# Opening loads in one queue, dummy matmuls in the opening, and a reordered last store in an adapter and mixture-of-experts kernel

## The chip, the cores and the metric

The kernel runs on one core of one Trainium2 chip. A core has five engines that run beside each other: TensorE (PE) for matrix products, VectorE (DVE), ScalarE (ACT), GpSimd (POOL) and SyncE (SP), which here only issues transfers, and 16 DMA engines that move the data. The metric is the device time of one execution in microseconds (us); less is better.

## What is computed

4,096 tokens (16 batches of 256, width 256) pass through an adapter that each batch chooses by an id, a layer norm, a shared feed-forward block and a mixture of eight experts, of which each token uses two. Cut to what matters:

```python
z = relu(einsum('bsh,bhk->bsk', x, down_w[ids]) + down_b[ids])
y = x + einsum('bsk,bkh->bsh', z, up_w[ids]) + up_b[ids]
h = (y - mean(y)) * rsqrt(var(y) + 1e-5) * ln_g[ids] + ln_b[ids]

def mlp(x, w1, b1, w2, b2):            # 256 -> 1024 -> 256
    return gelu(x @ w1 + b1) @ w2 + b2

p = softmax(h @ gate_w + gate_b)       # 8 experts
values, indices = top_k(p, 2)          # then divided by their sum
moe = sum over the two experts of value * mlp_e(h)
out = x + h + mlp_shared(h) + moe
```

All inputs and outputs are float32. The kernel gets float32 accuracy from f16 matmuls by splitting every operand into a high and a low part and multiplying three of the four pairs.

## The kernel before

**Stages.** For each batch `b`, the adapter computes z (L865, two f32 products), relu (L875), up (L881, and L885 for the bias row) and y (L896); `adapter_ln` does the layer norm (L922 to L961), `payload` splits the result into two f16 parts (L984, L989), transposes them on PE (L1000) and copies them to `xlnT` (L1008), and multiplies by the gate weights (L1019). `route` finds the two experts of each token for two batches at a time, and POOL scatters their rows into `xslot` in DRAM (L1139, 64 scatters). Beside that, `shared` runs the shared expert for one batch after another: 8 groups of 6 matmuls with W1 (L689), gelu on ACT (L696), a split into parts (L704 or L706, and L710), 8 groups of 6 matmuls with W2 (L725), and an eviction that adds to `base` (L1392). 13 of the 16 batches are done before the experts, the last three after them. The experts follow in units of 256 tokens: 16 at fixed places (two for each expert), then 16 whole and 5 half ones whose expert is found at run time. Each unit's blocks come by transposing loads on SP (L1281), and its weighted results are added to `yacc` in DRAM by POOL (L1303). At the end `yacc` is loaded back (L1607), added to `base` (L1627) and stored (L1615), batch by batch.

**Weights.** `Prep` loads one expert's f32 weights in two halves of about 1 MB (`load`, L539), sums their squares on ACT (L555), adds these up across partitions on PE (L578), computes scales on DVE (L585 to L603), and writes the scaled f16 high parts on ACT (L638) and the low parts on DVE (L644). `pE` is the `Prep` of the shared expert; its result is `wsh`. In the opening its two halves are issued from ACT's queue, after the load of adapter weights of batch 0 and of batch 1.

**The order of the work.** Nothing is ordered by hand. Every step is a `plan.op` with an engine, an assumed duration, a due time `v`, the steps that it needs (`deps`), steps that have to start before it (`after`), and buffers that it takes and gives back. `Plan.schedule` goes through a planned time: of all steps that are ready it takes the one that can start first, and among equals the one due first. The kernel then emits all steps in that order, so each engine's queue has a fixed order, and an engine stands still while the step at the head of its queue waits. The planned time is only used for the order. Due times come from a few numbers: `PACE` (start and step of the adapters, start and step of the shared units), `P_V` (the first two experts' weights), `VE2` (the shared expert's second half), `TV` and `WV` (how long before a unit its blocks and its weights are due), `PU2` (step of the expert units).

**The opening.** `load_batch` issues four loads of 256 KB for a batch from SP: the transposed input `xT` (L842), the adapter weights (L832, whose address comes from the id), the input `x` (L849) and the rows for the layer norm (L839). ACT's queue has the bias rows, the ids, the tables `gb_t` and `gw32` of the layer norm and the gate, the gate's bias and the shared expert's weights. `x_scales` turns the maxima of these tables into scales; it uses PE twice (transpose L470, spread L481). `constants` starts with 28 matmuls of a tile of ones into a bank of PSUM (`N_WARM`, L316).

Of the kernel before, what the change touches and what calls it, by code (L numbers as in the profile page):

```python
# [19 lines left out]
P = 128  # L20
NB = 16
# [3 lines left out]
E = 8  # L25
# [4 lines left out]
BLK = 256  # L30
# [25 lines left out]
X_FROM = 5  # L56
HALF_AT = (2, 5, 8, 11, 14)
# [91 lines left out]
P_V = (100.57, 91.12)  # L149
PACE = (0.0, 10.1, 24.89, 16.04)  # L150
VE2 = 3.67
TV, WV, PU2, VP = 9.48, 22.84, 10.68, 1.4
# [3 lines left out]
def adapter_moe_kernel(  # L156
# [16 lines left out]
    V, ACT, PE, POOL, SP = nc.vector, nc.scalar, nc.tensor, nc.gpsimd, nc.sync  # L173
# [15 lines left out]
    base = const([P, NTILE, D], F32, "base")  # L189
# [325 lines left out]
    class Prep:  # L515
# [29 lines left out]
        def build(self, joint=True, bank_of="pt"):  # L545
# [85 lines left out]
            for h, o in ((0, O_W1), (1, O_W2)):  # L631
                his = []
                for i in range(2):
# [17 lines left out]
                    his.append(plan.op("ACT", 1.1, hi, vh, [t[h], *sq[h:]] + gate[h]))  # L651
# [165 lines left out]
    z_of, ln_done, tc_done, lo_of, gate_of = {}, {}, {}, {}, {}  # L817
# [40 lines left out]
    def adapter_pe(b):  # L858
# [4 lines left out]
        def z():  # L863
# [7 lines left out]
            "PE", 0.86, z, va, [ld["xT"][b], ld["wa"][b]], acq=[("pt", ("z", b))], lat=0.3  # L871
# [21 lines left out]
        )  # L893
        return plan.op(
# [452 lines left out]
    gbl = plan.op("ACT", 0.45, lambda: ACT.dma_start(gb_t, lngb), 0.03, land=P * 128)  # L1347
    gwl = plan.op("ACT", 0.45, lambda: ACT.dma_start(gw32, gate_w), 0.03, land=P * 64)
    hot_first, hot_all = profile_rows()
    load_batch(0, 0.0, [])  # L1350
    pE = Prep(E, 2.3, after=[gwl], v2=VE2)
    pE.ld = [pE.load(0, 0.25, "ACT")]
    pE.ld[0]["after"] = [ld["wa"][0]]
# [4 lines left out]
    pE.ld.append(pE.load(1, 1.5, "ACT"))  # L1358
    pE.ld[1]["after"] = [pE.ld[0], ld["wa"][1]]
# [254 lines left out]
    def store(b, eng=SP):  # L1614
        eng.dma_start(  # L1615
            out[b * S : (b + 1) * S, :].rearrange("(t p) d -> p t d", p=P),
            base[:, 2 * b : 2 * b + 2, :],
        )
# [6 lines left out]
    def sum_y(b):  # L1625
        bb = base[:, 2 * b : 2 * b + 2, :]
        V.tensor_tensor(bb, bb, y_buf[b], ALU.add)  # L1627

    for b in range(NB):
        ld_y = plan.op(  # L1630
            "SP", 0.5, lambda b=b: y_load(y_buf[b], 2 * b, 2), v_end + b,
            [sc_last[NU - 1], *ring_free], land=P * 2048,
        )
        o = plan.op(
            "DVE", 0.69, lambda b=b: sum_y(b), v_end + 4.0 + 1.5 * b,
            [ld_y] + (last_evac[b] if b < NSH else []),
        )
        plan.op("SP", 0.5, lambda b=b: store(b), v_end + 9.0 + 1.5 * b, [o, *last_evac[b]])

    order = plan.schedule()  # L1640
    with tc.manual_schedule():
        constants()
        for o in order:
            o["fn"]()
# [117 lines left out]
```

## Time and profile before

| | |
|---|---|
| median of three runs | 628.97 us (628.46 to 629.08) |
| the profiled execution, its own time | 629.32 us |
| span in its profile, first to last instruction | 627.5 us |
| granted TensorE clock over the span, mean | 0.974 |
| PE busy | 599.8 us (96%) |
| DVE busy | 402.6 us (64%) |
| ACT busy | 412.3 us (66%) |
| POOL busy | 327.9 us (52%) |
| one group of six matmuls, L689 or L725, at full clock | about 0.66 us |
| DMA traffic | 129.30 MB, mean 206 GB/s |

In the profile an engine is busy while one of its instructions runs; PE's matmuls are pipelined. "PEclk" is the share of full speed that PE's clock was granted. The "chain that ended last" is followed back from the last instruction, at each step to what released it. A pair such as `wst<-in_adp_dram` is destination and source of an operation, without buffer numbers: `wst` also holds the adapter weights and rows in the opening. "SPq" and "ACTq" are the sequencers that issue transfers.

### The profile page before, as it was taken

Reading aid. Unit: us, or ns where it says so; the run is one execution under the profiler, and the core shown is the slowest. Engines: PE = TensorE matmul, PEld = TensorE weight load, DVE = VectorE, ACT = ScalarE, POOL = GpSimd, SP = SyncE. Lnnn points to the kernel's source line nnn. Section 1 sums busy time; section 2 is a strip of 40 time slices with the busy share of each in tenths; the row PEclk is TensorE's granted clock in tenths of the full one; section 3 lists DMA queues with packets and bytes.
Section 4 is the critical chain, followed back from the end, with each engine's and each line's share of the span. In section 5 each row is a group of like instructions: output and inputs, shape, how many; then the busy total and the mean of one; then the engine's idle time right before and its main releaser. Section 6 shows DMA issues by size and latency. Waiting matters only on the chain.

```text
span 627.5 us, 15396 instructions
## 1 busy us (share of the span) xinstructions
PE 599.8 (96%) x5541; PEld 521.1 (83%) x5541; DVE 402.6 (64%) x1005; ACT 412.3 (66%) x627; POOL 327.9 (52%) x541
## 2 busy tenths in 40 slices
PE   4799999999999999999999999999999999999993
PEld 3478877887888888888888888898898989889882
DVE  5698879898985338667777743444554555444464
ACT  1378765878787578788898766665565566555550
POOL 2005775662688326648446648564545844846300
PEclk7589999999999999999999999999999999999998
DMA  7856765975733378599999999656997499783297
GB/s 256 282 219 234 250 170 203 339 269 187 281 116 111 57 165 196 101 287 283 201 235 311 211 318 228 183 68 199 268 242 195 62 304 210 187 202 38 33 302 240
DMA packets 100315, 129.30 MB, mean 206 GB/s; under 512 B 56558, under 2 KB 83846, under 8 KB 92038
## 3 DMA queue, kind: packets, MB, share of 16 engines
q1 hardware_dynamic: 84210, 108.08, 58.6%
q0 software_dynamic: 15216, 18.01, 16.0%
q10 hardware_dynamic: 804, 2.16, 1.0%
q8 instruction: 45, 0.74, 0.5%
q14 instruction: 40, 0.33, 0.2%
HBM read 92.41 MB, written 46.58 MB: 222 GB/s over the span
## 4 chain that ended last, share of the span: by engine, by line
PE 87%; ACT 4%; DVE 4%; DMA 2%; issue 1%; SPq 0%; ACTq 0%; DVEq 0%
PE bank L689 40%; PE bank L725 40%; PE bank L881 3%; PE bank L865 2%; DMA wst<-in_adp_dram 1%; DVE base L1627 1%; PE bank L885 1%; PE bank L1000 1%; ACT h L696 1%; DVE hh L710 1%; DMA wst<-in_rows_dram 1%; PE bank L1019 1%; ACT wst L638 1%; ACT wsh L638 1%; ACT hh L704 1%
## 5 line engine op out<-in xcount | busy, mean ns | idle before, releaser
L725 PEld LDWEIGHTS <-hh 128*128 128x128 f16 x2424 | 235.0, 98 | 28.7 <-DVE hh L710 1.4
L696 ACT ACTIVATE h<-bank,tst 128x256 f32<-128x256 f32 x256 | 138.6, 559 | 107.9 <-PE bank L689 105.6
L725 PE MATMUL bank<-wst,hh 128*128 128x256 f16 x1536 | 206.5, 273 | 0.0
L689 PE MATMUL bank<-late,wst 128*128 128x256 f16 x1536 | 203.3, 273 | 1.2 <-ACT h L696 1.2
L1303 POOL DMA_INDIRECT yacc<-late,idt x69 | 124.3, 1801 | 128.7 <-DVE late L1544 23.7
L689 PEld LDWEIGHTS <-wst 128*128 128x128 f16 x1536 | 150.1, 98 | 18.8 <-issue 1.5
L1139 POOL DMA_INDIRECT xslot<-late,sli x64 | 73.5, 1148 | 86.0 <-DMA wst<-in_adp_dram 48.2
L710 DVE SCALAR_TENSOR_TENSOR hh<-h,tst,hh 128x1024 f16<-128x1024 f32 x64 | 82.1, 1283 | 36.6 <-ACT hh L704 35.8
L696 ACT ACTIVATE h<-bank,tsh 128x256 f32<-128x256 f32 x128 | 70.4, 561 | 50.3 <-PE bank L689 48.2
L689 PE MATMUL bank<-xlnT,wsh 128*128 128x256 f16 x768 | 102.7, 273 | 0.6 <-ACT h L696 0.6
L725 PE MATMUL bank<-wsh,hh 128*128 128x256 f16 x768 | 102.3, 273 | 0.9 <-DVE hh L710 0.9
L1294 POOL DMA_INDIRECT wq<-wtab,idt x69 | 78.5, 1137 | 40.0 <-DMA idt<-xslot 27.9
L689 PEld LDWEIGHTS <-wsh 128*128 128x128 f16 x768 | 74.2, 98 | 10.7 <-issue 1.1
L1288 DVE SCALAR_TENSOR_TENSOR late<-bank,tst 128x256 f32<-128x256 f32 x64 | 30.9, 483 | 68.9 <-PE bank L725 68.8
L704 ACT ACTIVATE hh<-h,tst 128x1024 f16<-128x1024 f32 x45 | 51.6, 1147 | 1.3
L710 DVE SCALAR_TENSOR_TENSOR hh<-h,tsh,hh 128x1024 f16<-128x1024 f32 x32 | 40.8, 1278 | 12.1 <-ACT hh L704 11.9
L704 ACT ACTIVATE hh<-h,tsh 128x1024 f16<-128x1024 f32 x30 | 34.4, 1147 | 0.8
L1302 POOL MEMSET spot<- 128x1 f32 x69 | 32.5, 471 | 0.0
L706 DVE TENSOR_SCALAR hh<-h,tst 128x1024 f16<-128x1024 f32 x19 | 14.7, 772 | 27.5 <-ACT h L696 27.5
L1544 DVE TENSOR_SCALAR late<-late,wq 128x256 f32<-128x256 f32 x69 | 25.6, 371 | 2.0
L1392 DVE SCALAR_TENSOR_TENSOR base<-bank,tsh,base 128x256 f32<-128x256 f32 x32 | 15.3, 480 | 16.0 <-PE bank L725 15.9
L644 DVE SCALAR_TENSOR_TENSOR wst<-wf,prep,wst 128x1024 f16<-128x1024 f32 x20 | 24.9, 1279 | 0.9 <-ACT wst L638 0.9
(225 smaller groups left out, 599.6 us busy)
## 6 DMA issues: line engine op xcount, KB each, us to landing
wst<-scr SPq DMA_DIRECT2D x32, 1024.0 KB
scr<-wst SPq DMA_DIRECT2D x16, 1024.0 KB
wf<-scr SPq DMA_DIRECT2D x10, 1024.0 KB
wf<-in_ew_dram SPq DMA_DIRECT2D x5, 1028.0 KB
wf<-in_ew_dram SPq DMA_DIRECT2D x5, 1024.0 KB
wst<-in_adp_dram SPq DMA_DIRECT2D x16, 256.5 KB
xlnT<-in_xT_dram SPq DMA_DIRECT2D x16, 256.0 KB
base<-in_x_dram SPq DMA_DIRECT2D x16, 256.0 KB
```

Source lines behind the costliest of these rows:

```text
L644: V.scalar_tensor_tensor(self.w[:, a + 2048 : b + 2048], self.wf[h][:, f], sc[:, 2 * h : 2 * h + 1], self.w[:, a:b], ALU.mult, ALU.subtract,)
L689: mm = PE.matmul(pa[:, 0:n_tok], w1[:, wl, c, k, :], xin[:, xl, k, 0:n_tok], start=i == 0, stop=i == len(seq) - 1,)
L696: ACT.activation(h32[:, c % 4, 0:n_tok], pa[:, 0:n_tok], AF.Gelu_apprx_tanh, bias=tail[:, c : c + 1], scale=tail[:, 8:9],)
L704: ACT.activation(hi, h4, AF.Copy, scale=tail[:, 9:10])
L710: V.scalar_tensor_tensor(hh[:, 1, c, 0:n_tok], h32[:, :, 0:n_tok], tail[:, 9:10], hh[:, 0, c, 0:n_tok], ALU.mult, ALU.subtract,)
L725: PE.matmul(py, hh[:, hl, k, t * P : (t + 1) * P], w2[:, wl, k, :], start=q == 0 and i == 0, stop=q == 3 and i == len(seq) - 1,)
L1139: ins = POOL.indirect_dma_start(out=xslot[:, :], out_offset=bass.IndirectOffsetOnAxis(ap=sli[:, c, j : j + 1], axis=0), in_=payb[plan.slot ...
L1288: V.scalar_tensor_tensor(ysb, py, tail[:, 10:11], tail[:, 11 : 11 + D], ALU.mult, ALU.add)
L1294: POOL.indirect_dma_start(out=wq[:, t : t + 1], out_offset=None, in_=wtab[:, :], in_offset=bass.IndirectOffsetOnAxis(ap=idt[:, t, 0:2].bit ...
L1302: POOL.memset(spot, 0.0)
L1303: ins = POOL.indirect_dma_start(out=yacc[:, :], out_offset=bass.IndirectOffsetOnAxis(ap=idt[:, t, 2:4].bitcast(I32), axis=0), in_=ysb, in_ ...
L1544: lambda: V.tensor_scalar(ysb(), ysb(), wqb[plan.slot["wq", s]][:, t : t + 1], None, ALU.mult), v, [ty, wq_of[s, t]], rel=[("wq", s)] if t ...
```

## The change

The change sets new numbers for the due times and does the following.

- The shared expert's two halves go to SP's queue: the first behind the adapter weights and rows of batch 0, the second behind the rows of batch 1. `gb_t` and `gw32` become due first on ACT's queue.
- z of batch 1 may be placed only behind up of batch 0.
- The high parts of a `Prep` no longer name the sums of squares as steps that they need; they need the scales alone, and those of the first half come from the first sum (in `pE`, where the halves have scales of their own).
- While the steps are emitted, before every PE step whose planned start is under 45 us, three matmuls of ones into bank 4 are put for each microsecond of PE's planned gap.
- At the end the loads of `yacc` are assumed shorter and the sums due later; the sum of the last batch has to come before its two evictions, and that batch is stored in two halves, each behind its own eviction.

```diff
+FILL_END, FILL = 45.0, 3.0
...
-P_V = (100.57, 91.12)
-PACE = (0.0, 10.1, 24.89, 16.04)
-VE2 = 3.67
-TV, WV, PU2, VP = 9.48, 22.84, 10.68, 1.4
+P_V = (86.01, 98.41)
+PACE = (0.0, 9.44, 26.24, 15.04)
+VE2 = 5.01
+TV, WV, PU2, VP = 16.73, 16.8, 10.65, 1.4
...
-                    his.append(plan.op("ACT", 1.1, hi, vh, [t[h], *sq[h:]] + gate[h]))
+                    his.append(plan.op("ACT", 1.1, hi, vh, [t[h]] + gate[h]))
...
         z_of[b] = plan.op(
-            "PE", 0.86, z, va, [ld["xT"][b], ld["wa"][b]], acq=[("pt", ("z", b))], lat=0.3
+            "PE", 0.86, z, va, [ld["xT"][b], ld["wa"][b]], acq=[("pt", ("z", b))], lat=0.3,
+            after=[up_of[0]] if b == 1 else [],
         )
...
+        up_of[b] = up_
...
-    gbl = plan.op("ACT", 0.45, lambda: ACT.dma_start(gb_t, lngb), 0.03, land=P * 128)
-    gwl = plan.op("ACT", 0.45, lambda: ACT.dma_start(gw32, gate_w), 0.03, land=P * 64)
+    gbl = plan.op("ACT", 0.45, lambda: ACT.dma_start(gb_t, lngb), -0.5, land=P * 128)
+    gwl = plan.op("ACT", 0.45, lambda: ACT.dma_start(gw32, gate_w), -0.5, land=P * 64)
     hot_first, hot_all = profile_rows()
     load_batch(0, 0.0, [])
-    pE = Prep(E, 2.3, after=[gwl], v2=VE2)
-    pE.ld = [pE.load(0, 0.25, "ACT")]
-    pE.ld[0]["after"] = [ld["wa"][0]]
+    pE = Prep(E, 2.1, after=[gwl], v2=VE2)
+    pE.ld = [pE.load(0, 0.25)]
+    pE.ld[0]["deps"], pE.ld[0]["after"] = [], [ld["rw"][0], ld["wa"][0]]
...
-    pE.ld.append(pE.load(1, 1.5, "ACT"))
-    pE.ld[1]["after"] = [pE.ld[0], ld["wa"][1]]
+    pE.ld.append(pE.load(1, 1.5))
+    pE.ld[1]["deps"], pE.ld[1]["after"] = [], [pE.ld[0], ld["rw"][1]]
...
-            [sc_last[NU - 1], *ring_free], land=P * 2048,
+            [sc_last[NU - 1], *ring_free], land=P * 1400,
...
-            "DVE", 0.69, lambda b=b: sum_y(b), v_end + 4.0 + 1.5 * b,
+            "DVE", 0.69, lambda b=b: sum_y(b), v_end + 6.0 + 2.3 * b,
...
-        plan.op("SP", 0.5, lambda b=b: store(b), v_end + 9.0 + 1.5 * b, [o, *last_evac[b]])
+        if b < NB - 1:
+            plan.op("SP", 0.5, lambda b=b: store(b), v_end + 9.0 + 1.5 * b, [o, *last_evac[b]])
+            continue
+        for t, e in enumerate(last_evac[b]):
+            e["after"].append(o)
+            plan.op(
+                "SP", 0.5,
+                lambda b=b, t=t: SP.dma_start(
+                    out[(2 * b + t) * P : (2 * b + t + 1) * P, :], base[:, 2 * b + t, :]
+                ), 1e4, [o, e],
+            )
+
+    def idle_pe(n):
+        pw = bank[4][:, 0:BLK]
+        for _ in range(n):
+            PE.matmul(pw, ones, ones.unsqueeze(1).broadcast_to([P, 2, P]), start=True, stop=True)
 
     order = plan.schedule()
     with tc.manual_schedule():
         constants()
+        at = 6.0
         for o in order:
+            if o["eng"] == "PE" and o["start"] < FILL_END:
+                idle_pe(max(0, int((o["start"] - at) * FILL)))
+                at = max(at, o["start"] + o["durs"][o["engs"].index("PE")])
             o["fn"]()
```

More of the change, by code (lines that the diff above doesn't have):

```diff
@@ L816, in adapter_moe_kernel @@
     ld = {"x": {}, "xT": {}, "wa": {}, "rw": {}}
-    z_of, ln_done, tc_done, lo_of, gate_of = {}, {}, {}, {}, {}
+    z_of, ln_done, tc_done, lo_of, gate_of, up_of = {}, {}, {}, {}, {}, {}
     def A(b):
```

## The prediction

> **What bounds the kernel now.** I read four views in this order: the page's 40 slices, the chain that ended last, the busy time by stretches, and the same chain's end.
>
> ```profile
> PE   4799999999999999999999999999999999999993
> ...
> DVE  5698879898985338667777743444554555444464
> ...
> PEclk7589999999999999999999999999999999999998
> DMA  7856765975733378599999999656997499783297
> ```
>
> A slice is 15.7 us. TensorE (PE) is full from the fourth slice to the last but one; it is short only in the first three, where its granted clock is low too, and in the last. So the kernel is an opening, a long body in which PE sets the pace, and an end. From 200 to 600 us PE is busy 398.85 of 400. What the change can win lies in front of that body and behind it.
>
> ```profile
> 7.47 8.55 DMA wst<-in_adp_dram
> 16.16 2.05 PE bank L865 x4
> 18.72 1.15 PE bank L881 x2
> 20.19 1.15 PE bank L881 x2
> 21.70 0.69 DVE base L896
> 28.79 1.99 ACT wsh L555 x2
> 30.77 0.91 ACT xlnT L1008
> 31.68 1.42 ACT wsh L638 x2
> 33.66 2.17 ACT wsh L638 x2
> ...
> 38.61 0.76 PE bank L689 x6
> ```
>
> This is the chain's start (start, us, what). The adapter weights of batch 1, issued at 7.47, land at 16.02. PE takes its work in order, so z of batch 1 (L865) stands at the head, and up of batch 0 (L881) behind it, though batch 0's relu was done at 11.47 + 0.47 = 11.94. From 38.61 on PE is continuous; the first matmul of the shared expert (L689) ran at 34.59.
>
> ```profile
> core 0: us, PE busy (x) PEld busy (x) DVE busy (x) ACT busy (x) POOL busy (x), PEclk, DMA share, GB/s
> 4.71:8.12 3.41, 1.35 (x12) 0.96 (x10) 2.19 (x11) 0.00 (x0) 0.00 (x0) 1.00 0.81 231
> ...
> 11.53:14.95 3.42, 0.00 (x0) 0.00 (x0) 0.00 (x0) 0.42 (x1) 0.00 (x0) 0.50 1.01 407
> ...
> 18.36:21.77 3.41, 3.41 (x9) 1.64 (x10) 1.08 (x8) 2.24 (x3) 0.00 (x0) 0.50 1.02 362
> ...
> 32.01:35.43 3.42, 3.42 (x23) 2.60 (x22) 2.85 (x7) 3.42 (x4) 0.00 (x0) 0.50 0.11 16
> ```
>
> The clock is full until 8.12 and half from there to 35.43. In 11.53:14.95 PE and VectorE (DVE) do nothing while the DMA engines are full: the opening waits for bytes in the wrong order.
>
> ```profile
> 617.50 0.68 DVE base L1627
> 618.17 0.41 DVE base L1392
> 618.60 0.69 DVE base L1627
> ```
>
> The end: the last eviction (L1392), then the last sum (L1627), then a store. But the stretches say that the DMA engines are the other limit there: share 1.08 in 615.65:619.06, and 1.02, 0.71, 0.97, 1.07, 0.61 in the five microseconds from 618 to 623.
>
> **The change, part by part.** *z of batch 1 behind up of batch 0, and the order of loads.* Up of batch 0 could start at 12.0 and started at 18.65: 6.6 us. The spread matmul (L481, 0.58 us), whose operand was ready at 11.47, comes free with it and takes some of the gap back: 6.2. z of batch 0 also stood behind the transpose L470, which waited for the gate weights until 9.29; these are now first on ACT's queue, and z can start when its own weights are there, near 9.0: another 0.4. So the first y (L896, 21.70) comes at about 15.1, 6.6 earlier. From y to the end of the transposed copy of batch 0 (L1008, 30.68 + 1.00) took 31.68 - 21.70 = 10.0 us; kept as it is, that copy is there at 25.1.
>
> *Shared weights.* The halves of 1 MB leave ACT's queue. On SP's they cost two issues of some 0.4 us, hidden, as SP next waits for landings anyway. Ahead of the first half lie batch 0's loads and xT of batch 1, 1.3 MB, which were through by about 9; 1.05 MB at the 403 GB/s of 10:15 is 2.6 us, so it lands near 12.5. Square (L555) 1.9 + 0.2 gives 14.6; from its total (L578, 25.94) to the scales (L603, 28.80) took 2.9: 17.5; two scaled copies (L638) of 1.13: 19.8; the second remainder (L644) 1.28: 21.1. So W1 is ready before xlnT, where now its copies start at 31.58, since they wait for the Square of the second half at 28.79. That wait is what the removed dependency on sq frees; what is late next is xlnT. The first shared matmul can start at 25.1, not 34.59: -9.5.
>
> *What of that reaches the body.* DVE's work is only moved. It is busy 5.00 of 5.00 in 25:30, 4.35 and 4.96 in the next two stretches, and begins 6.6 earlier, not 9.5. So the start of the continuous stretch moves by 6.6 (DVE decides) to 9.5 (xlnT decides). DVE had 0.65 us idle between 30 and 35 while it waited for the copies on ACT, which now come early; I take **7.5**.
>
> *Dummy matmuls.* FILL is 3 for each planned microsecond of gap. The 28 warm-up matmuls of the same shape took 4.99, 0.178 each, so at most half of a gap is filled, directly behind the operation before it. PE was idle some 12 us between 6 and 35, so 12 x 3 x 0.178 = 6.4 us of dummies lie in idle time; that idle time hides them. If a gap of 3 us is planned and isn't there, they hold PE up by 9 x 0.178 = 1.6. What they can win is the clock: z took 1.98 at half clock and 1.03 at full (42.85), up 3.01 against 1.75: 2.2 on batch 0's path. The clock fell after 1.35 of 3.41 busy and, at the end, held after 1.76 of 3.41 (615.65:619.06), so dummies that bring a stretch to half full could keep it. Ends: +2.0 (no clock, a gap missing) and -2.2; I take **0.5** gained, as one gap missing eats most of it.
>
> By the Trainium skill, "TensorE: Matmul & The Clock Gate", Part 1, one busy window of about 3.4 us releases the clock and one idle window throttles it. The trace disagrees with the first half: 18.36:21.77 shows PE busy 3.41 of 3.41, and the clock stayed at 0.50 until 35.43, so records of f32 matmuls don't count as full.
>
> *Loads, queue against queue.* While 1 MB each of W1 and W2 ran on ACT's queue, batch 1's 256 KB took 8.55 us. Behind each other in one queue the same bytes need no more time in all (383 to 403 GB/s between 10 and 20), and batch 1 is whole near 14 instead of 17.4; that only feeds y of batch 1, inside the 7.5.
>
> The Trainium skill, "DMA: Bandwidth & Descriptors", "Issuing engines are not separate DMA queues", speaks against this part: the queues share the same 16 engines, and several issuers only save issue time. By it the move would gain nothing, and the sum would keep the 6.6 of the order on PE; the 8.55 us row says that sharing does delay the smaller transfer.
>
> *The body.* The new due times (PACE, P_V, TV, WV, PU2) move no work in or out; I cost them at 0. The cover: the last routing scatter ran at 203.1, the first expert block's two transposing loads were issued at 206.22 and 208.95, its first matmul ran at 216.91, and shared work lasted to 224.8. DVE, POOL and the loads start earlier with the rest. If the routing didn't come along, PE would run out near 217 and wait about 4 us in the first unit's own chain.
>
> *The end.* Sum before eviction takes 0.69 (L1627) off the path, and halves let the first 128 KB go one eviction (0.99) sooner. The last store was issued at 620.20; it could go at about 618.8. But of the 5 us from 618 the DMA engines were busy 4.38, and no byte is saved; only the hole in 619:620 (0.29) and a shorter last transfer go. Ends: -1.3 and +1.0 (DVE now holds the last eviction for the last y load, issued at 610.20); I take **-0.4**. The sum waits for nothing else, and behind it in DVE only the two evictions stand.
>
> Sum: -7.5 - 0.5 - 0.4 = -8.4. The profiled execution took 629.32 (span 627.5 and 1.8 around it), so 620.9; the median is 0.35 below it: **620.5**.
>
> **Rivals.** *Clock kept full from 4.7 on.* For it: 1.76 of 3.41 sufficed to hold it. Against: the dummies stand in a lump at a gap's head. Opening -9.5 - 2.2, end -0.4: 629.0 - 12.1 = 616.9.
>
> *Routing doesn't follow.* For it: 64 scatters in series on POOL, to 203.1, with PE waits near 190. Against: POOL is only 53 to 64% busy from 100 to 300. 620.5 + 4 = 624.5.
>
> *The order that it says isn't the order that counts:* up of batch 0 gains, but DVE, 85 to 99% busy in most stretches of 50 to 190, swallows it. Against: DVE begins earlier as well. 628.9.
>
> *Slower: weights late behind blocks on SP.* The unit at 406.55 has its weights issued at 399.87 and 400.56; two loads of 1 MB need 5.3 us at 390 GB/s, so little is spare. Weights were due 22.84 ahead and blocks 9.48; now 16.80 and 16.73. SP waits for PE before transposing loads 54.9 us in all, 7.5 at longest; a weight load behind such a wait comes up to 7.5 late. Of the reloads in the dynamic units (issues of 0.33 us; skipped ones take 0.08) one lies 6.7 before its use, three about 9.6 and three about 12: 6.5 + 3 x 3.4 + 3 x 1 = 20 us at worst, half of it 10: 630.5. It decides from 8.4 us of PE waits between 350 and 570; against it: weights go out as a buffer frees, and PE waited 0.6 from 250 on.
>
> **How the numbers follow.** Forecast 0.68, full clock 0.11, routing 0.06, swallowed 0.04, slower 0.11. The forecast's own range: -9.5 - 2.2 - 1.3 gives 616, -6.6 + 2.0 + 1.0 gives 625.4. The range 615.5 to 628.0 takes in all but the last two cases and a little beyond the best. A measurement here tells 0.2% (1.3 us) from no change. Faster: 0.68 + 0.11 + 0.06, less 0.01 for a poor forecast; same 0.04; slower 0.12.
>
> **What would show it.** Up of batch 0 near 12, first L689 near 25, PE continuous from about 31; the clock back at 1.00 before 32; copies L638 of W1 before the second Square; the last L896 and all later stages some 8 earlier; the end, from last scatter's landing to the last instruction, as long as now (32 us) less 0.4. Wrong would be: L865 of batch 1 again ahead of L881, dummies next to a late L578, or PE waits over 1 us behind 350.

## The result, and the profile after

The changed kernel took 626.58 us in the median of 8 runs (622.15 to 627.90), the kernel before, beside it, 629.03: ratio 0.9953, 95% interval 0.9931 to 0.9975. It is faster by 2.45 us, where I had forecast 8.5, and the forecast of 620.5 is 6 us too low, though inside its range. The profiled execution was the best of the eight, 622.15 (span 620.3, mean clock 0.988). So what its profile shows is what the change can give; what it usually gives is read from further profiles of the same kernel.

Lines behind the edits are moved by 1 to 3: L689 is now L690, L725 L726, L865 L866, L881 L883, L896 L899, L1008 L1011, L839 L840, L955 L958; the dummies are L1656. Some experiments move them by up to two more. First the 40 slices of the page, 15.5 us each:

```profile
PE   7999999899999999999999999999999999999993
...
DVE  7979878788966554776886644445545455455474
...
PEclk9799999899999999999999999999999999999998
DMA  7987879648522388599999799747998489792397
```

PE is full from the second slice on, and the clock is low in one slice of the opening (7). Before, PE was full from the third slice, not from the fourth as I had read it, and the clock was low in three (7, 5, 8). But the eighth slice, from 109 to 124 us, now has an 8 in the rows PE and PEclk where the kernel before had 9. Busy time by stretches of the opening (same columns as in the prediction: length, then busy time of PE, weight loads, DVE, ACT, POOL with counts, granted clock, DMA share, GB/s):

```profile
4.71:8.12 3.41, 2.59 (x21) 1.84 (x19) 1.61 (x13) 0.00 (x0) 0.00 (x0) 1.00 0.82 227
...
11.53:14.95 3.42, 2.02 (x9) 1.18 (x9) 2.51 (x7) 1.85 (x2) 0.00 (x0) 1.00 1.01 391
...
18.36:21.77 3.41, 3.41 (x16) 1.91 (x15) 2.46 (x5) 2.91 (x3) 0.00 (x0) 0.50 1.06 378
32.01:35.43 3.42, 3.42 (x19) 2.01 (x19) 2.61 (x8) 3.02 (x5) 0.00 (x0) 1.00 0.49 28
```

In 11.53:14.95, where PE and DVE stood still before, both work, and 32.01:35.43 is at full clock. The half clock is down from 27.3 us to 6.8. And the timeline (start, duration, engine, line, result and operands, idle time before it and its releaser):

```profile
9.20 1.10 PE L866 MATMUL bank<-xlnT,wst 128*128 128x256 f32 x4 [1.27 <-DMA wst<-in_adp_dram]
...
10.90 0.66 PE L883 MATMUL bank<-wst,zT 128*128 128x256 f32 x2
...
13.79 0.69 DVE L899 TENSOR_TENSOR base<-bank,base 128x512 f32<-128x512 f32 x1 [0.33 <-PE bank L887]
14.28 1.41 PE L866 MATMUL bank<-xlnT,wst 128*128 128x256 f32 x4 [0.32 <-DMA wst<-in_rows_dram]
...
19.99 1.28 DVE L645 SCALAR_TENSOR_TENSOR wsh<-wf,prep,wsh 128x1024 f16<-128x1024 f32 x1
...
21.58 1.28 DVE L645 SCALAR_TENSOR_TENSOR wsh<-wf,prep,wsh 128x1024 f16<-128x1024 f32 x1
...
24.44 0.75 DVE L992 SCALAR_TENSOR_TENSOR late<-base,sx,late 128x512 f16<-128x512 f32 x1
...
26.77 1.02 ACT L1011 ACTIVATE xlnT<-bank 128x1024 f16<-128x1024 f16 x1
...
28.16 0.82 PE L690 MATMUL bank<-xlnT,wsh 128*128 128x256 f16 x6
```

Up of batch 0 runs at 10.90, ahead of z of batch 1 at 14.28, and the first sum is there at 13.79, 7.9 earlier than before. The transposed copy of batch 0 then takes 12.98 us from that sum, not 8.98 (21.70 to 30.68), so the first shared matmul is 6.4 earlier, at 28.16, not 9.5. Between the two stand the remainders of W1 on DVE (the two L645 above). In the kernel before, they came behind that copy:

```profile
33.21 2.47 DVE L644 SCALAR_TENSOR_TENSOR wsh<-wf,prep,wsh 128x1024 f16<-128x1024 f32 x2
```

The stretch around the new hole, from the stretches, the waits of DVE and PE, and the timeline of the transfers that SP issues:

```profile
113.90:117.30 3.40, 3.31 (x48) 2.70 (x45) 0.00 (x0) 3.40 (x6) 2.44 (x6) 1.00 1.06 397
117.30:120.70 3.40, 0.69 (x7) 0.62 (x8) 2.97 (x10) 1.73 (x2) 0.00 (x0) 1.00 0.47 180
120.70:124.20 3.50, 3.50 (x16) 2.10 (x14) 3.50 (x24) 1.28 (x2) 0.00 (x0) 0.51 0.02 5
```

```profile
DVE base L958 <- DMA wst<-in_rows_dram: 4.0, 1, 4.0
...
PE bank L726 <- DVE hh L711: 2.8, 1, 2.8
```

```profile
96.12 0.34 SPq L670 DMA_DIRECT2D scr<-wst  x1
...
99.70 0.52 SPq L670 DMA_DIRECT2D scr<-wst  x1
100.26 0.92 SPq L540 DMA_DIRECT2D wf<-in_ew_dram  x2
102.49 2.46 SPq L833 DMA_DIRECT2D wst<-in_adp_dram  x2
105.00 1.21 SPq L1470 DMA_DIRECT2D yacc<-in_x_dram  x2
109.98 1.81 SPq L840 DMA_DIRECT2D wst<-in_rows_dram  x2
```

DVE does nothing from 113.7 to 117.7: the norm step L958 at the head of its queue waits for rows that SP issued from 109.98 on. Ahead of them went two stores of 1 MB of expert 0's finished weights, 2 MB of expert 1's raw weights (L540 at 100.26), and copies into `yacc`; the DMA engines are full until 117. Behind L958 in DVE's queue stands the low part of a shared unit (L711), for which PE waits 2.8 us; the clock is then half for one window, 120.7 to 124.2. In the kernel before, the rows went out ahead of the 2 MB:

```profile
110.29 0.36 SPq L839 DMA_DIRECT2D wst<-in_rows_dram  x1
...
112.68 0.35 SPq L839 DMA_DIRECT2D wst<-in_rows_dram  x1
...
117.51 3.28 SPq L539 DMA_DIRECT2D wf<-in_ew_dram  x2
```

The end, in the timeline and in stretches of 1 us:

```profile
607.63 2.49 DVE L1630 TENSOR_TENSOR base<-base,wst 128x512 f32<-128x512 f32 x4
610.22 0.88 DVE L1395 SCALAR_TENSOR_TENSOR base<-bank,tsh,base 128x256 f32<-128x256 f32 x2
612.46 1.81 SPq L1648 DMA_DIRECT2D out_dram<-base  x2
```

```profile
610.00:611.00 1.00, 0.50 (x5) 0.20 (x3) 0.90 (x3) 0.00 (x0) 0.00 (x0) 1.00 1.09 382
611.00:612.00 1.00, 0.00 (x0) 0.00 (x0) 0.10 (x1) 0.00 (x0) 0.00 (x0) 1.00 1.09 382
...
614.00:615.00 1.00, 0.00 (x0) 0.00 (x0) 0.00 (x0) 0.00 (x0) 0.00 (x0) 1.00 1.02 349
```

All engines are done at 611.1, 0.6 us behind the last matmuls, and the DMA engines then write for another 4 us at a full share: the sum and the eviction were moved, the bytes were not.

### The profile page after: what moved, and what is told of

It is laid out like the page before. It is cut to its first block, busy times and chain, and to the rows that moved or that the text cites. A ratio compares the mean times of both kernels' runs of the same rounds, so it can differ in the third digit from the quotient of the medians.

```text
span 620.3 us, 15463 instructions
## 1 busy us (share of the span) xinstructions
PE 600.1 (97%) x5575; PEld 521.8 (84%) x5575; DVE 400.0 (64%) x1004; ACT 412.5 (67%) x628; POOL 326.7 (53%) x541
## 4 chain that ended last, share of the span: by engine, by line
## 5 line engine op out<-in xcount | busy, mean ns | idle before, releaser
L726 PEld LDWEIGHTS <-hh 128*128 128x128 f16 x2424 | 234.8, 98 | 32.5 <-DVE hh L711 4.6
L726 PE MATMUL bank<-wst,hh 128*128 128x256 f16 x1536 | 206.9, 273 | 0.4 <-DVE hh L711 0.4
L690 PE MATMUL bank<-late,wst 128*128 128x256 f16 x1536 | 203.3, 273 | 0.0
L690 PEld LDWEIGHTS <-wst 128*128 128x128 f16 x1536 | 150.1, 98 | 17.3
L1142 POOL DMA_INDIRECT xslot<-late,sli x64 | 71.3, 1113 | 80.4 <-issue 56.5
L726 PE MATMUL bank<-wsh,hh 128*128 128x256 f16 x768 | 103.4, 274 | 3.9 <-DVE hh L711 3.4
L711 DVE SCALAR_TENSOR_TENSOR hh<-h,tst,hh 128x1024 f16<-128x1024 f32 x64 | 82.1, 1283 | 38.1 <-ACT hh L705 37.2
L690 PE MATMUL bank<-xlnT,wsh 128*128 128x256 f16 x768 | 103.2, 273 | 0.0
L1297 POOL DMA_INDIRECT wq<-wtab,idt x69 | 80.8, 1172 | 32.5 <-DMA idt<-xslot 20.5
L690 PEld LDWEIGHTS <-wsh 128*128 128x128 f16 x768 | 73.7, 98 | 10.1
L711 DVE SCALAR_TENSOR_TENSOR hh<-h,tsh,hh 128x1024 f16<-128x1024 f32 x32 | 40.8, 1280 | 7.3 <-ACT hh L705 7.1
L1305 POOL MEMSET spot<- 128x1 f32 x69 | 32.1, 465 | 0.0
L707 DVE TENSOR_SCALAR hh<-h,tst 128x1024 f16<-128x1024 f32 x19 | 14.6, 768 | 26.3 <-ACT h L697 26.3
L645 DVE SCALAR_TENSOR_TENSOR wst<-wf,prep,wst 128x1024 f16<-128x1024 f32 x20 | 25.3, 1278 | 0.1
L1296 POOL MEMSET spot<- 128x1 f32 x69 | 25.0, 362 | 0.0
```

What stands on the lines that cost most here:

```text
L645: V.scalar_tensor_tensor(self.w[:, a + 2048 : b + 2048], self.wf[h][:, f], sc[:, 2 * h : 2 * h + 1], self.w[:, a:b], ALU.mult, ALU.subtract,)
L690: mm = PE.matmul(pa[:, 0:n_tok], w1[:, wl, c, k, :], xin[:, xl, k, 0:n_tok], start=i == 0, stop=i == len(seq) - 1,)
L711: V.scalar_tensor_tensor(hh[:, 1, c, 0:n_tok], h32[:, :, 0:n_tok], tail[:, 9:10], hh[:, 0, c, 0:n_tok], ALU.mult, ALU.subtract,)
L726: PE.matmul(py, hh[:, hl, k, t * P : (t + 1) * P], w2[:, wl, k, :], start=q == 0 and i == 0, stop=q == 3 and i == len(seq) - 1,)
L1142: ins = POOL.indirect_dma_start(out=xslot[:, :], out_offset=bass.IndirectOffsetOnAxis(ap=sli[:, c, j : j + 1], axis=0), in_=payb[plan.slot ...
L1297: POOL.indirect_dma_start(out=wq[:, t : t + 1], out_offset=None, in_=wtab[:, :], in_offset=bass.IndirectOffsetOnAxis(ap=idt[:, t, 0:2].bit ...
```

## How the profiles are compared

A kernel's profile is one execution, and medians from different chips differ (the kernel before had medians of 628.8 to 633.2 us). So besides the ratios, each taken against the kernel before on the same chip, I use one figure from every profile: what PE loses in a stretch. It is the idle time (length less PE's busy time) plus the length times (1 less the granted clock). For 113.90:117.30 to 120.70:124.20 above this gives 0.1 + 2.7 + 1.7 = 4.5 us.

"Opening and end" in the table is the difference of the spans to the kernel before (627.5) less the difference of the losses in 45:600 (3.5 there); it charges to the opening and the end whatever the body doesn't explain.

| kernel | ratio | z of batch 0 | first sum | sum to copy | first shared matmul | lost in 100:140 | lost in 45:600 | opening and end |
|---|---|---|---|---|---|---|---|---|
| before | 1 | 9.46 | 21.70 | 8.98 | 34.59 | 0.0 | 3.5 | 0 |
| before, b1_before | | 9.14 | 21.07 | 8.98 | 33.59 | 0.0 | 4.6 | -0.7 |
| changed | 0.9953 | 9.20 | 13.79 | 12.98 | 28.16 | 4.4 | 5.9 | -9.6 |
| changed, e1_again | 0.9986 | 10.39 | 15.25 | 13.27 | 30.55 | 6.5 | 11.3 | -6.5 |
| changed, e5_again | 0.9955 | 11.94 | 17.00 | 13.27 | 32.31 | 2.9 | 4.4 | -5.1 |
| rows first, e6_rows | 0.9890 | 12.02 | 17.57 | 13.25 | 32.86 | 0.0 | 2.6 | -4.5 |
| rows first, e7_again | 0.9909 | 11.20 | 17.31 | 12.73 | 32.09 | 0.0 | 4.3 | -3.2 |
| rows first, e9_again | 0.9950 | 9.02 | 15.26 | 13.17 | 29.83 | 0.6 | 9.7 | -3.8 |

The last six have one and the same opening and end, and give 3.2 to 9.6 for it, 5.5 in the mean, where the forecast had 8.4 (e3_pv below, with the same opening and end, gives 3.7). One caution goes with all experiments: the planner orders all work anew after every edit. An edit of the opening therefore changes the order in the body too, and a median holds both. Which stretch lost the time is read from the profile, which is one execution and not the median.

## Experiments: the body

**Theory A**: the new `P_V` puts 2 MB of expert weights ahead of row loads that the layer norm needs soon, in the one queue of SP. **Rivals**: the opening gained little in the usual run; or another of the due times costs.

*e1_again*, the changed kernel unaltered.

> The changed kernel once more, unaltered. Its eight executions spread from 622.15 to 627.9 us, while those of the kernel before stay within 1.7 us, and the one with a full trace was the fastest. Theory A (late rows): the opening's gain of some 7 us is there in every execution, and most of it is lost again where the layer norm waits for its rows (L840) behind 2 MB of expert weights on the same queue, between 95 and 130 us, 4 us in the fast execution and more in the others. A expects the typical execution at 626 to 628 with PE continuous from about 26 us as in the traced one, and one or more PE stalls of together 6 us or more between 90 and 200. Theory B (clock): the opening itself differs from execution to execution, since the dummies do not always keep the clock; B expects the first L690 or the continuous stretch some 4 us later than in the traced one (28.2), and no longer stall behind 60 us.

Measured: 632.06 (10 runs), ratio 0.9986, interval 0.9952 to 1.0021. The profile has the same wait for the rows, 4.1 us on DVE and 2.9 on PE, and two windows at half clock behind it: 6.5 us lost in 100:140. The first shared matmul comes at 30.55, 2.4 later than in the first profile, so a part of the first rival holds too: the opening differs from execution to execution.

*e3_pv*, only `P_V` set back.

```diff
-P_V = (86.01, 98.41)
+P_V = (100.57, 91.12)
```

> Only P_V set back to (100.57, 91.12): the first two experts' weights are due in the old order, and in SP's queue a pair of row loads then stands ahead of the 2 MB of weights instead of behind it. A: the wait for rows near 118 goes, PE idle between 100 and 200 falls by 3 us or more, and the time comes to 619 to 623 with a small spread. B: no change within 1 us, 626 to 627.5.

Measured: 627.25 (4 runs), ratio 0.9872, interval 0.9797 to 0.9948: faster than the changed kernel on the same chip by 4.8 us, though four runs leave a wide interval. In the profile nothing is lost in 100:140 and the wait for the rows is gone.

*e4_olddue*, all due times set back; the opening's order, the dummies and the end stay.

```diff
-P_V = (86.01, 98.41)
-PACE = (0.0, 9.44, 26.24, 15.04)
-VE2 = 5.01
-TV, WV, PU2, VP = 16.73, 16.8, 10.65, 1.4
+P_V = (100.57, 91.12)
+PACE = (0.0, 10.1, 24.89, 16.04)
+VE2 = 3.67
+TV, WV, PU2, VP = 9.48, 22.84, 10.68, 1.4
```

> All due times (PACE, P_V, VE2, TV, WV, PU2) set back, with the new order of loads, z behind up, dummies and end. A: the opening's gain stays (first L690 before 30), and stalls in 90 to 200 depend on the old order, which had 2.3 us of them: 620 to 624. B: as the changed kernel, 626 to 627.5. If the due times carry the opening's gain, it is near 629.

Measured: 626.56 (7 runs), ratio 0.9916, interval 0.9879 to 0.9953. With all due times set back the kernel is not told apart from the one with `P_V` alone set back, as the two intervals overlap: a gain of the other due times is not shown.

*e5_again* and *e6_rows* then ran on one chip: the changed kernel unaltered, and the same with one more condition: expert 1's weights may not be placed ahead of the row loads of batch 12.

```diff
-    prep[1] = Prep(1, P_V[1], after=[z_of[7]])
+    prep[1] = Prep(1, P_V[1], after=[z_of[7], ld["rw"][12]])
```

> The changed kernel unaltered, as the yardstick for the two beside it on the same chip. If what was seen so far holds, PE stalls once behind the split of a shared unit (L726 waiting for DVE L711) near 118 to 122 us, because DVE waits 4 us for rows (L958 on in_rows), and the clock halves for one or two windows of 3.4 us after it. Time 1 to 3 us under the kernel before.

> The changed kernel, but the second expert's weights may be placed only behind the rows of batch 12; in SP's queue the four row loads then stand ahead of these 2 MB. All due times stay as changed. Theory A (late rows): DVE's 4 us wait for rows and the PE stall behind it go, no half clock after the opening before 300 us, and the time falls by 3 to 6 us under the changed kernel on the same chip. Rival C (the new due times as a whole put too much work for DVE and ACT into 100 to 150, the rows are only where it shows): the wait moves to another place, less than 1.5 us is won.

Measured: 627.22 (12 runs), ratio 0.9955, interval 0.9933 to 0.9978; and 622.19 (6 runs), ratio 0.9890, interval 0.9854 to 0.9925. The stretch 100:140 in e5_again and in e6_rows:

```profile
100.00:140.00 40.00, 37.15 (x335) 30.06 (x335) 32.90 (x109) 29.81 (x43) 20.16 (x49) 1.00 0.69 256
```

```profile
100.00:140.00 40.00, 40.00 (x376) 32.87 (x374) 34.93 (x126) 26.36 (x42) 20.23 (x49) 1.00 0.79 276
```

And SP's issues in e6_rows:

```profile
113.81 1.51 SPq L840 DMA_DIRECT2D wst<-in_rows_dram  x2
...
125.82 0.34 SPq L840 DMA_DIRECT2D wst<-in_rows_dram  x1
126.21 0.91 SPq L540 DMA_DIRECT2D wf<-in_ew_dram  x2
```

PE is busy 40.00 of 40.00. The rows go out later than in the changed kernel (113.81 against 109.98), but with no 2 MB ahead of them they land 3.5 us after their issue and not 7.7, and the norm step L958 that needs them runs at 117.48 without a wait. Theory A holds, at 5.0 us on this chip. Two more measurements of this kernel elsewhere, e7_again and e9_again below, gave 0.9909 and 0.9950; over three measurements each the means are 0.9965 with the stall and 0.9916 without, which is 3.1 us. The wait is gone in all of them; how much of it reaches the end varies. The clock has a part in that: DVE waited 4.0 to 4.1 us and PE 2.8 to 2.9 in all three profiles of the changed kernel, but one window of 3.41 us at half clock followed in the first, two in e1_again and none in e5_again, hence the 4.4, 6.5 and 2.9 us of the table.

*b2_pvnew* and *b1_before*: the kernel before with the new `P_V` alone, and unaltered for its profile on that chip.

```diff
-P_V = (100.57, 91.12)
+P_V = (86.01, 98.41)
```

> The kernel before with one of the changed numbers, P_V = (86.01, 98.41): the 2 MB of the next expert then stand ahead of the row loads of batches 11 and 12 on SP's queue here too. A: a wait of DVE for rows appears between 100 and 135 us, PE stalls 2 to 4 us, and it is 2 to 5 us slower than the kernel before. C: without the other new due times the same order costs less than 1 us.

> The kernel before, for its trace on the same chip as the three others: first L689 near 34.6, clock at half from about 8 to 35, no wait for rows between 100 and 150, and no stall over 1 us behind 250. Should it stall behind 250 here as the changed kernel did on the last chip near 335 (ACT 4 us without an instruction), that stall is the chip's and not the change's.

Measured: 631.49 (12 runs), ratio 1.0035, interval 1.0014 to 1.0055; b1_before 629.63. So `P_V` costs on the kernel before too, 2.2 us, but not by the rows. The profile of b2_pvnew has this at 130:

```profile
129.84 4.25 ACT L638 ACTIVATE wst<-wf,prep 128x1024 f16<-128x1024 f32 x4
...
134.00 1.00 ACT L1008 ACTIVATE xlnT<-bank 128x1024 f16<-128x1024 f16 x1
...
135.06 0.46 PE L1019 MATMUL bank<-gw,xlnT 128*128 128x8 f16 x12 [2.64 <-ACT xlnT L1008]
```

Four scaled copies of expert 1 stand ahead of a batch's transposed copy on ACT; PE waits 2.64 us for that, and the clock is half from 136.3 to 143.1. The same number that made the rows late in one order made ACT late in another. What carries over is that `P_V` moves 2 MB and some 8 us of ACT's work into a stretch that had no slack, and not the place where it shows.

## Experiments: the opening and the end

*e2_nofill*, the changed kernel without dummies, on the chip of e1_again; and *e7_nofill*, the kernel of e6_rows without them, on that of e7_again.

```diff
-FILL_END, FILL = 45.0, 3.0
+FILL_END, FILL = 45.0, 0.0
```

> FILL = 0: no dummy matmuls, all else as changed; the plan is the same. A: the opening is at half clock until about 30 us, which costs 1.5 to 3 us there, the later stalls are as they are: 627 to 630, and the spread remains. B: without dummies every execution has the late opening, so about 627 and with a small spread, no slower than the changed kernel's typical execution.

> The kernel with the row loads ahead of the 2 MB, unaltered once more, as the yardstick for the other three on this chip. If the late rows were the one large loss, it stays about 5 us faster than the changed kernel was and 1.1% faster than the kernel before: ratio 0.985 to 0.993.

> The same, with no dummy matmuls in the opening's gaps. By my prediction's term 0.5 us slower than the yardstick. The look at the changed kernel without them gave first shared matmuls 3.5 us later in one profiled execution, but no slower median: so theory A says 2 to 4 us slower now that the stall on the rows no longer covers it, half clock from about 8 to 35 us; rival B says within 0.7 us, the dummies' gain being lost in the placing of the clock's windows.

Measured: e2_nofill 631.23, ratio 0.9959, interval 0.9927 to 0.9992 (e1_again: 0.9986); e7_nofill 624.42, ratio 0.9922, interval 0.9903 to 0.9942; e7_again 624.54, ratio 0.9909, interval 0.9887 to 0.9931. In neither pair is there a difference that the intervals show. The profiles of e7_again and of e7_nofill fit that:

```profile
17.00:27.20 10.20, 7.24 (x42) 4.70 (x41) 9.85 (x37) 5.63 (x7) 0.00 (x0) 1.00 1.02 348
27.20:34.00 6.80, 6.80 (x40) 4.58 (x40) 5.53 (x22) 4.03 (x5) 0.00 (x0) 0.50 0.60 101
```

```profile
17.00:27.00 10.00, 6.77 (x18) 3.86 (x16) 8.62 (x36) 5.64 (x7) 0.00 (x0) 0.50 0.97 334
27.00:34.00 7.00, 7.00 (x39) 4.48 (x39) 5.32 (x20) 3.97 (x5) 0.00 (x0) 0.50 0.50 109
```

With dummies the clock is full from 17.0 to 27.2, but there DVE is busy 9.85 of 10.20 and sets the pace; when the shared expert starts and PE sets it, the clock is half again until 34.0, as it is without them. The first shared matmul ran at 32.09 and 32.12.

*e7_zfirst*, the kernel of e6_rows with z of batch 1 ahead of up of batch 0, loads left in one queue.

```diff
-            after=[up_of[0]] if b == 1 else [],
+            after=[],
         )
+        if b == 1:
+            up_of[0]["after"].append(z_of[1])
```

> The same, but z of batch 1 is put ahead of up of batch 0 on TensorE again, which then waits for batch 1's adapter weights; the loads stay in one queue. By my prediction's chain, y of batch 0 comes about as late as z of batch 1 allows: z of batch 1 starts at 14 to 18 here, so the first sum comes 2.5 to 5 us later than in the yardstick, and the kernel is 2 to 4 us slower (the first shared matmul as much later). Rival: DVE has other work to do first (the copies of W1), and the order of these two steps is worth under 1 us now.

Measured: 623.41, ratio 0.9900, interval 0.9879 to 0.9921. The rival holds in the time. In the profile z of batch 1 ran at 14.84, since its weights come early in the one queue, the first sum at 18.58 (17.31 in e7_again), the first shared matmul at 31.75 (32.09). Some of that is chance: z of batch 0 ran at 10.00 here and at 11.20 in e7_again, so counted from there the sum came 2.5 us later.

*e8_act*, the loads of the opening as before, z of batch 1 still behind; *e8_actz*, both orders as before. Both on the kernel of e6_rows.

```diff
-    pE.ld = [pE.load(0, 0.25)]
-    pE.ld[0]["deps"], pE.ld[0]["after"] = [], [ld["rw"][0], ld["wa"][0]]
+    pE.ld = [pE.load(0, 0.25, "ACT")]
+    pE.ld[0]["after"] = [ld["wa"][0]]
...
-    pE.ld.append(pE.load(1, 1.5))
-    pE.ld[1]["deps"], pE.ld[1]["after"] = [], [pE.ld[0], ld["rw"][1]]
+    pE.ld.append(pE.load(1, 1.5, "ACT"))
+    pE.ld[1]["after"] = [pE.ld[0], ld["wa"][1]]
```

(The due times of `gb_t` and `gw32` go back to 0.03 as well; e8_actz adds the edit of e7_zfirst.)

> The kernel with the row loads ahead of the 2 MB (ratio 0.989 and 0.991 to the kernel before in two calls), with the loads of the opening as before: the shared weights' halves on ScalarE's queue, the gate weights later; z of batch 1 stays behind up of batch 0. By my prediction the order on TensorE carries the gain (6.6 of 7.5 us) and the loads little: ratio stays at 0.989 to 0.993, first shared matmul within 1 us of the yardstick's 32. Rival: the loads' order carries it, and this is back near 0.997 to 1.000, with the copies of W1 late again (after 25 us).

> The same, and z of batch 1 ahead of up of batch 0 as well, so that both orders of the opening are those of before. By my prediction y of batch 0 comes at 21 us again and the kernel is 4 to 7 us slower than e8_act: ratio 0.997 to 1.002. If it stays at 0.990, neither order gives anything and what is gained over the kernel before lies behind the opening, in the due times or in the freed dependency of the W1 copies.

Measured: 632.32, ratio 0.9996, interval 0.9960 to 1.0032; and 638.58, ratio 1.0081, interval 1.0044 to 1.0119. The order on TensorE is worth 0.85% here, some 5 us, and shows where it should: first sum at 13.64 against 21.71, first shared matmul at 28.99 against 34.01. By the table's reckoning 4.8 us of the difference between these two profiles lie in the opening and the end; 4.3 more are lost in the body, most of it in 360:600 of e8_actz. So where the loads are in one queue, the order on TensorE adds nothing that the time shows, and where they are in two, it does. e8_act's own opening is not worse than that of the changed kernel (28.99 lies within 28.16 to 32.86). Its ratio is, and its profile shows a loss of 8.0 us in 140:205:

```profile
140.00:205.00 65.00, 60.25 (x556) 50.23 (x554) 48.48 (x172) 48.75 (x69) 43.26 (x98) 0.95 0.45 162
```

The kernels with rows first lose 1.2 to 2.0 there, but on other chips; all four kernels of this chip lose 4.3 to 8.0 there, and rows first was not measured beside them. So whether the body came out in a worse order, or the chip has a part in it, is not shown, and whether the loads' order as such is worth anything is left open.

*e8_sq*, the copies of W1 wait for both Squares again, and *e8_lo*, the two remainders of W1 go behind the low part of batch 0's copy. Both on the kernel of e6_rows.

```diff
-                    his.append(plan.op("ACT", 1.1, hi, vh, [t[h]] + gate[h]))
+                    his.append(plan.op("ACT", 1.1, hi, vh, [t[h], *sq[h:]] + gate[h]))
```

```diff
+    for o in pE.los:
+        o["after"].append(lo_of[0])
     scats = []
```

(Two more lines of e8_lo keep these steps in `los`; the edit of e8_sq is in the code of every `Prep`.)

> The kernel with the row loads ahead, but the copies of W1 wait for the Squares of both halves again. By my prediction W1 is ready long before the transposed copy of batch 0 and there is slack: the second Square ended at 24.3 to 26 in the looks so far, the copies would end 4.5 us later, and the first shared matmul moves from 32 to about 31 to 33: within 1 us of the yardstick, ratio 0.988 to 0.993. Rival: the early copies are what fills VectorE before batch 0's norm; with them later the norm comes 2.5 us sooner and this is faster by up to 2 us. Third: W1 becomes the last to come and it is 2 to 3 us slower.

> The kernel with the row loads ahead, but VectorE takes the two remainders of W1 (2 x 1.28 us) behind the low part of batch 0's transposed copy, not ahead of its norm. From the first sum to the transposed copy took 9.0 us in the kernel before and 13.0 to 13.3 in every look at the changed one. If the remainders ahead of it are the cause, this shrinks to 10 to 11 and the transposed copy comes 2 to 3 us sooner; the first shared matmuls then wait for the remainders instead, so the time gains 0 to 2 us. If the cause is batch 1's norm between, it stays at 12 to 13 and nothing is gained.

Measured: e8_sq 630.82, ratio 0.9960, interval 0.9922 to 0.9998; e8_lo 626.82, ratio 0.9921, interval 0.9883 to 0.9959. In both the way from first sum to transposed copy shrinks from about 13 to 10.27 us: the remainders of W1 are most of what lengthened it; the 1.3 us that are left against the kernel before are not explained. In e8_lo the copy starts at 25.19 and the first shared matmul at 28.39. In e8_sq the copy starts at 27.44 and W1 is last, its second remainder done at 29.46; the first shared matmul comes only at 33.44, but until then PE runs z and up of later batches, at half clock, and doesn't wait for W1. From first sum to first shared matmul it takes 16.3 us in e8_sq, 14.6 to 15.3 with rows first and 13.5 in e8_lo. So the price of the freed dependency is shown, that DVE took the early work first; what it gains is 1 to 2 us in these profiles, and the two intervals of the times overlap.

*e7_tail*, the kernel of e6_rows with the end of the kernel before.

```diff
-        if b < NB - 1:
-            plan.op("SP", 0.5, lambda b=b: store(b), v_end + 9.0 + 1.5 * b, [o, *last_evac[b]])
-            continue
...
+        plan.op("SP", 0.5, lambda b=b: store(b), v_end + 9.0 + 1.5 * b, [o, *last_evac[b]])
```

(The assumed length of the loads of `yacc` and the due times of the sums go back as well.)

> The same, with the end of the kernel before (last batch evicted first, then summed, stored in one piece). By my prediction's term for the end (0.4 us) this is 0.4 us slower than the yardstick, which this measurement hardly sees. Rival: the term's end of -1.3 us holds, and it is 1.3 slower. Other rival: the eviction held for the last y load costs, and the old end is up to 1 us faster. To be read from the last matmul to the end of the span: yardstick less than the old end by 0.4 (by my term), 1.3, or more by 1.0.

Measured: 622.44, ratio 0.9891, interval 0.9872 to 0.9909; e7_again 0.9909. From the 4,601st of the 4,968 matmuls of the two shared lines to the end of the span it took 50.6 to 51.2 us in the four profiles with the old end (mean 50.9) and 49.6 to 51.4 in the sixteen with the new one (mean 50.6).

*e9_wflo*, the edit of e8_lo, and the first 1 MB of shared weights behind the adapter weights of batch 1 in SP's queue; *e9_again*, the kernel of e6_rows beside it.

```diff
     load_batch(1, 0.9, [])
+    pE.ld[0]["after"].append(ld["wa"][1])
```

> The kernel with the row loads ahead of the 2 MB once more, as the yardstick for the other run: ratio 0.987 to 0.993 to the kernel before, z of batch 0 starting anywhere from 9.2 to 12.2 us as in the looks so far, 13.0 to 13.3 us from the first sum to the transposed copy of batch 0.

> The remainders of W1 behind the low part of batch 0's copy (as in e8_lo), and the first 1 MB of shared weights one adapter load later in SP's queue, behind batch 1's. Theory: the 1 MB directly behind batch 0's adapter weights in one queue delays their last packets, since in all 12 looks with that order z of batch 0 started between 9.2 and 12.2 us, and in the 5 with the 1 MB on the other queue between 9.05 and 9.75; so here it starts between 9.0 and 9.8, and the first shared matmul 1 to 2 us sooner than in the yardstick, with the copy 2 us sooner again. Ratio 0.984 to 0.990. Rival: the late z is only the phase of the transfers' start, z stays between 9.2 and 12.2, and the ratio is the yardstick's within 0.002.

Measured: e9_again 628.42 (10 runs), ratio 0.9950, interval 0.9927 to 0.9973, outside what I had expected; its profile loses 9.7 us in 45:600, of it 2.9 in 45:100. e9_wflo 622.79 (6 runs), ratio 0.9856, interval 0.9822 to 0.9891: the fastest kernel of the study, 5.6 us ahead of the one beside it. Its opening:

```profile
8.72 1.10 PE L868 MATMUL bank<-xlnT,wst 128*128 128x256 f32 x4 [0.94 <-DMA wst<-in_adp_dram]
...
13.64 0.69 DVE L901 TENSOR_TENSOR base<-bank,base 128x512 f32<-128x512 f32 x1 [1.19 <-PE bank L889]
...
24.42 2.47 DVE L645 SCALAR_TENSOR_TENSOR wsh<-wf,prep,wsh 128x1024 f16<-128x1024 f32 x2
...
24.99 1.02 ACT L1013 ACTIVATE xlnT<-bank 128x1024 f16<-128x1024 f16 x1 [1.69 <-PE bank L1005]
...
26.85 0.81 PE L692 MATMUL bank<-xlnT,wsh 128*128 128x256 f16 x6
```

z of batch 0 at 8.72, the copy 11.35 behind the first sum, the first shared matmul at 26.85, 7.7 ahead of the kernel before; by the table's reckoning 7.5 us from opening and end. This is the size that the forecast had for the changed kernel. Whether the place of the 1 MB or the order on DVE gave more of it is not settled: z came at 9.02 in e9_again too, without the edit.

## Why the prediction was wrong

The opening moved the way that was forecast; the sum did not come out. By the means above, and so as an estimate, the 6 us between 620.5 and 626.58 come from two places of about the same size: 3.1 in the body, and 2.9 in the opening and the end (8.4 forecast, 5.5 measured).

**The step that failed: "The body. The new due times (PACE, P_V, TV, WV, PU2) move no work in or out; I cost them at 0."** The cover that I named was the distance from the routing to the first expert block, near 210. What the due times moved was the preparation of experts 0 and 1, at 96 to 126, in a stretch where SP's queue also carries the adapters' loads. The runs showed 2.9 to 6.5 us lost in 100:140 in each of three profiles, none in the kernel before, and 3 to 5 us in the medians. A rival of mine had late weights in SP's queue, but behind 350, where blocks and weights alternate; there PE lost 0.4 to 0.8 us from 360 to 600 in the three profiles of the changed kernel, and that rival fell.

**The opening, sized too large: -7.5 and -0.5, measured with the end 5.5 in the mean of six profiles (3.2 to 9.6).**
- *Up of batch 0 first.* Forecast first sum at 15.1; measured 13.79 to 17.57. "z can start when its own weights are there, near 9.0" held in two profiles of six; in the others z came at 10.4 to 12.0.
- *"kept as it is, that copy is there at 25.1"*. It was not kept: 12.7 to 13.3 us instead of 9.0 (10.0 with the copy itself). I had W1 ready at 21.1, ahead of the copy, and took "DVE's work is only moved", without putting its 2 x 1.28 us on DVE ahead of batch 0's norm; in the kernel before they stood behind the copy. This is shown by e8_lo and e8_sq, which take them away from there and win some 3 of the 4 us back.
- *Shared weights.* Right: Square at 13.10 (forecast 12.5), copies of W1 at 17.19 (17.5), second remainder done at 22.9 (21.1), in the first profile.
- *Dummies.* Forecast 0.5, measured nothing in two pairs. The rival with the clock kept full fell too: 6.8 us at half clock remain in the opening of the best profile, 13.7 in that of e7_again.
- *Loads on one queue.* "that only feeds y of batch 1, inside the 7.5": it also took most of what the order on TensorE was to bring (e7_zfirst), and the 6.6 us for that order are shown only with the loads in two queues (e8_act and e8_actz). The Trainium skill, "DMA: Bandwidth & Descriptors", "Issuing engines are not separate DMA queues", by which the move gains no time in the transfers, is not contradicted by e8_act, where the loads on two queues had the first shared matmul at 28.99.

**The end: -0.4**, measured -0.3 between means whose profiles scatter by 0.6 and 1.8; right in size and not to be told from nothing.

**Routing.** The last scatter ran at 200.5 against 203.1, 2.6 earlier and not 8; PE still lost nothing from 205 to 300, so the rival fell.

The order of up and z, W1's copies ahead of the second Square (17.19 against 19.28) and PE nearly continuous from 31 came as told. The clock was back before 32 in three of six profiles (21.8, 25.1 and 30.5, against 32.8 to 34.0). The hole at 117 was not on the list.

## What to carry to other kernels

A due time in a planned kernel is a place in a queue: before costing a change of such numbers at nothing, write down which transfers and which engine steps it passes, and who waits for those. Work that is made ready early is not free if it stands ahead of the critical step on a full engine; here 2.5 us of weights on DVE took back a third of what the new order had won. Two edits that both bring the same step forward are not to be added, and where a planner orders everything anew, an edit must be judged by its stretch of the trace as well as by the median.

## What the runs showed of the hardware

- The clock changes in steps of 3.41 us whose phase differs from run to run (the first full stretch began at 4.7 in the changed kernel, 5.5 in e5_again, 6.7 in e7_again). One window with PE busy 0.69 of 3.40 (117.30:120.70) was followed by one at half clock, and in e7_again one with 1.27 of 3.40 by two. 18.36:21.77, with 2.56 us of f16 dummies in it (from 19.21 on), was followed by full clock, where the same window in the kernel before, filled mostly by f32 matmuls, was not. So the rule of the Trainium skill, "TensorE: Matmul & The Clock Gate", Part 1, that one busy window releases the clock, agrees with the one and not with the other. Nor does PE's busy time alone say when the clock falls: a window with 1.72 us busy (e5_again, 121.50:124.92) was followed by full clock, one with 2.11 (e8_act, 164.92:168.34) by half. That puts in doubt the forecast's guess that dummies need only fill half of a window.
- A 256 KB load behind 2 MB and more in the same queue landed 7.7 us after its issue (109.98 to 117.71 in the changed kernel), in e6_rows without the 2 MB 3.5 us after it. And a 256 KB load with 1 MB directly behind it in the queue can end late: in e5_again the last of the 128 packets of batch 0's adapter weights ended at 11.03, 14 of them after 9.0, while packets of the 1 MB behind them were already moving in the same queue; in the kernel before, with the 1 MB in another queue, the last ended at 8.55. In 14 profiles with that order z of batch 0 started between 9.0 and 12.2, in five with the 1 MB in the other queue between 9.05 and 9.75, and in e9_wflo, with the 1 MB one load later, at 8.72. The cause is not shown.
- In e1_again ACT stood 4.1 us, from 330.2 to 334.3, while no buffer or operand was late by the profile; an 8 KB packet of instructions ran from 333.55 to 333.86, with the DMA engines at a share of 0.98 in 330:335. In the best profile of the changed kernel the same packet began at 327.4 and ACT did not stand. That the wait was for it is inferred.
